# Behind the second attention: normalisation on ScalarE, single banks for the MLP's first product, its differences at the end, Gelu's table at the start

## The chip, the cores and the metric

The kernel runs on one core of one Trainium2 chip. The metric is device time in microseconds, from several executions; a profiled execution comes with a trace of every instruction of the five engines (TensorE is PE, its weight loads PEld; VectorE is DVE; ScalarE is ACT; GpSimd is POOL; SyncE, SP, issues most transfers). Everything is float32.

## What is computed

An input of 16 images with 256 channels and 32x32 pixels, so 1024 tokens an image, goes through two layers. Cut to what matters:

```python
# layer 0: attention, 4 heads of 64, with a residual
qkv = xs @ w_proj + b_proj
x = softmax(q @ k.T * 64**-0.5) @ v @ w_out + b_out + xs
# layer 1: group_norm, attention with 8 heads of 32, group_norm, MLP
x = x + attention(group_norm(x, gn1_w, gn1_b))
h = group_norm(x, gn2_w, gn2_b)
h = gelu(mlp_w1 @ h + mlp_b1)          # 256 -> 1024
x = x + mlp_w2 @ h + mlp_b2            # 1024 -> 256
```

A group norm has 32 groups of 8 channels; the softmax runs without subtracting a maximum, and a check of the denominators at the end decides whether a general version has to run as well. It doesn't run with these inputs.

## The kernel before

**Layout.** Channels lie on the 128 partitions in two chunks (CC = 2), tokens along the free dimension in two halves of 512 (NT = 2). [...]three double tiles `s0`, `s1`, `s2` (`wide`, L289) and two single banks `b0`, `b1` (`bank`, L295). `wide` without a number takes the double tile that was used longest ago, except for those in `kept`.

**One image.** The loop at L1089 handles image b in two stages, and each stage also carries work of a neighbouring image:

- The first attention (`attention_a`, L376). It has four items, (query half t, channel chunk c), with eight key blocks each. For every key block PE makes scores (L390), ACT their exponentials (L398), PE the weighted values two blocks later (L411), and DVE adds the exponentials up (`es`, L423); the first tile of an item is held and added together with the second, so that an item has seven adds. At an item's end ACT copies one half of the result (L427) and DVE adds the other (L428). During the fourth item the scores alternate between `s0` and `s1`, since `s2` holds the item's result. When both items of a half are done, `normalise` (L435) makes the denominators on PE (`den_a`, L442), which go out to memory as a row, are inverted, and come back (`denominators`, L349); `scale` (L462) multiplies the result by them. `out_proj` (L652) follows: product, residual (L663) and statistics (L666).
- Within that stage, after the first half's denominators, comes the rest of the image before: the last projection of its second attention (`j`), the statistics, and the second `group_norm` (L690, key `h`). `averages` (L695) averages over a group by PE; `apply` (L730) makes a factor `a` and an offset `c` per channel and applies them by four DVE operations (L746), one per half and chunk. `sums_of_input` (L868) then makes five sums and differences of the four blocks on DVE (L875 to L879).
- After the attention, `hidden` (L945): the first product of the MLP of the image before. It uses seven products for a two-by-two block product where eight are usual (Strassen's way). For each i of four, `begin` makes products 2 and 5 in a double tile and product 1 in a bank of its own (`once`), ACT copies one with a minus (L923), DVE makes `rest` (L924, L925); `middle` adds products 4 and 3 and takes two Gelus; `finish` adds 7 and 6, DVE makes two units (L938, L939), ACT takes two Gelus (L911), and `combine` (L951, operation at L954) makes two differences of units. The parts run as begin 0, begin 1, middle 0, middle 1, finish 0, finish 1, and the same for 2 and 3. The first group norm of this image (key `g`) and the second half of its projection (`o`) lie between them.
- Then the first products of the second attention (`qkv_1`, L822) and the second attention (`attention_b`, L500), which is filled up with the remaining products of `qkv_1`, the MLP's second product of the image before (`outputs`, `reduce`, L974) and the first products of the next image. The differences of units are read there.

**Order.** Every engine works through a queue whose order is fixed before the kernel runs. A planner makes that order: it takes what is ready by its own reckoning of time, and of several ready instructions the one written earlier. `tc.keep_in_program_order` ties an instruction behind the one written before it on the same engine. `Later` (L31) delays the writing of a step by a number of steps of the loop, so that a result that is long in coming is not waited for. The variable `cols` (L331) is 32 while an attention is being written and 128 (P) outside it, so `cols[0] == P` tells the group norm `g`, and the very last `h`, from the other fifteen `h`.

Of the kernel before, what the change touches and what calls it, by code (L numbers as in the profile page):

```python
# [8 lines left out]
F32 = mybir.dt.float32  # L9
I32 = mybir.dt.int32  # L10
AF = mybir.ActivationFunctionType
ALU = mybir.AluOpType
AX = mybir.AxisListType

P = 128
# [223 lines left out]
def first_pass(ctx, tc, x, out, k):  # L239
    nc = tc.nc  # L240
    B, C, S = x.shape
# [6 lines left out]
    small = ctx.enter_context(tc.tile_pool(name="small", bufs=2))  # L248
# [36 lines left out]
    def use(n):  # L285
        order.remove(n)
        order.append(n)

    def wide(name, n=None):  # L289
        if n is None:  # L290
            n = next(m for m in order if m not in kept)
        use(n)
        return ps_s.tile([P, 2, TB], F32, tag=f"s{n}", name=name)

    def bank(name, n):  # L295
        return ps_a.tile([P, TB], F32, tag=f"b{n}", name=name)
# [34 lines left out]
    cols = [P]  # L331

    def product(o, w, r, **flags):
        for c0 in range(0, P, cols[0]):
            sl = slice(c0, c0 + cols[0])
            nc.tensor.matmul(o[sl], w[:, sl], r, **flags)  # L336
# [353 lines left out]
    def group_norm(key, src, stats, gw, gb, tag, out_tile, wait, then=None):  # L690
        st = {}

        def averages(name, src):  # L695
            if cols[0] == P:
                ps = bank(name, 1)
                product(ps[:, :CC], k["gavg"], src, start=True, stop=True)
                return [(slice(0, P), ps[:, :CC])]
            ps = wide(name)  # L700
            halves = [slice(h, h + HALF) for h in range(0, P, HALF)]
            for n, sl in enumerate(halves):
                nc.tensor.matmul(
                    ps[sl, n, :CC], k["gavg"][sl, sl], src[sl], start=True, stop=True
                )
            return [(sl, ps[sl, n, :CC]) for n, sl in enumerate(halves)]

        def means():
            mv = small.tile([P, CC, 2], F32, tag="mv", name=f"mv_{key}")
            for cc in range(CC):  # L710
                nc.vector.bn_aggr(mv[:, cc, :], stats[:, cc].rearrange("p t k -> p (t k)"))
            mean_c = small.tile([P, CC], F32, tag="mean_c", name=f"mean_c_{key}")
            nc.vector.tensor_copy(mean_c, mv[:, :, 0])
            st.update(mv=mv, mean_c=mean_c)
            later.after(wait, variances)

        def variances():
            mean = small.tile([P, CC], F32, tag="mean", name=f"mean_{key}")
            for sl, ps in averages(f"gm_{key}", st["mean_c"]):
                nc.vector.tensor_copy(mean[sl], ps)  # L720

            dv = small.tile([P, CC], F32, tag="dv", name=f"dv_{key}")
            nc.vector.tensor_sub(dv, st["mean_c"], mean)
            nc.vector.tensor_mul(dv, dv, dv)
            tv = small.tile([P, CC], F32, tag="tv", name=f"tv_{key}")
            nc.vector.tensor_add(tv, dv, st["mv"][:, :, 1])
            st.update(mean=mean, tv=tv)
            later.after(1 if cols[0] == P else 2, apply)

        def apply():  # L730
            rstd = small.tile([P, CC], F32, tag="rstd", name=f"rstd_{key}")
            for sl, ps in averages(f"gv_{key}", st["tv"]):
                nc.vector.tensor_scalar(rstd[sl], ps, EPS, None, ALU.add)
            nc.gpsimd.tensor_tensor(rstd, rstd, k["mhalf"], ALU.pow)
            a = small.tile([P, CC], F32, tag="ga", name=f"ga_{key}")
            nc.vector.tensor_mul(a, rstd, gw)
            ma = small.tile([P, CC], F32, tag="gma", name=f"gma_{key}")
            nc.vector.tensor_mul(ma, st["mean"], a)
            c = small.tile([P, CC], F32, tag="gc", name=f"gc_{key}")
            nc.vector.tensor_sub(c, gb, ma)  # L740
            y = act.tile([P, CC, S], F32, tag=tag, name=f"gn_{key}")
            out_tile.append(y)
            for t in range(NT):
                sl = slice(t * TB, (t + 1) * TB)
                for cc in range(CC):
                    nc.vector.tensor_scalar(  # L746
                        y[:, cc, sl], src[:, cc, sl],
                        a[:, cc : cc + 1], c[:, cc : cc + 1], ALU.mult, ALU.add,
                    )
            if then:  # L750
                then(y)

        means()
# [114 lines left out]
    def sums_of_input(b, y):  # L868
        extra = act.tile([P, 3, TB], F32, tag="hs", name=f"hs_{b}")
        y11, y12 = (y[:, 0, t * TB : (t + 1) * TB] for t in range(NT))  # L870
        y21, y22 = (y[:, 1, t * TB : (t + 1) * TB] for t in range(NT))
        s1, s6, s7 = (extra[:, n] for n in range(3))
        inputs[b] = {1: s1, 2: y11, 3: y12, 4: y21, 5: y22, 6: s6, 7: s7}
        todo = [
            lambda: nc.vector.tensor_add(s1, y11, y22),  # L875
            lambda: nc.vector.tensor_add(s7, y21, y22),
            lambda: nc.vector.tensor_sub(y21, y21, y11),
            lambda: nc.vector.tensor_add(s6, y11, y12),
            lambda: nc.vector.tensor_sub(y12, y12, y22),  # L879
        ]  # L880
        for n, fn in enumerate(todo):
            if b < B - 1:
                later.after(1 + n, fn)
            else:
                fn()

    def mlp(b, xb):
        n4 = HC // 2
        gs, open_sums = {}, {}
# [6 lines left out]
        def products_of(i, to):  # L896
            for number, ps, first in to:
                nc.tensor.matmul(  # L898
                    ps, blocks[1][number - 1][:, i * P : (i + 1) * P],
                    inputs[b][number], start=first, stop=True, skip_group_check=not first,  # L900
                )

        def unit(half, t, i):
            gs[half, t, i] = work.tile(
                [P, TB], F32, tag="g", name=f"g_{b}_{half}_{t}_{i}", bufs=16
            )
            return gs[half, t, i]

        def gelu(half, t, i, what):
            hc = half * n4 + i  # L910
            nc.scalar.activation(  # L911
                gs[half, t, i], what, AF.Gelu, bias=k["m1b"][:, hc : hc + 1]
            )

        def begin(i):
            ps = wide(f"m1_{b}_{i}")
            if i % 2 == 0:
                open_sums["once"] = wide(f"m1_{b}_{i}_1")
            once = open_sums["once"][:, i % 2, :]
            open_sums[i] = ps  # L920
            products_of(i, [(2, ps[:, 0, :], True), (5, ps[:, 1, :], True), (1, once, True)])
            minus, rest = unit(0, 1, i), unit(1, 1, i)
            nc.scalar.activation(minus, ps[:, 0, :], AF.Copy, scale=-1.0)  # L923
            nc.vector.tensor_sub(rest, minus, ps[:, 1, :])  # L924
            nc.vector.tensor_add(rest, rest, once)  # L925
# [8 lines left out]
        def finish(i):  # L934
            ps = open_sums.pop(i)
            products_of(i, [(7, ps[:, 0, :], False), (6, ps[:, 1, :], False)])
            rest = gs[1, 1, i]
            nc.vector.tensor_add(unit(0, 0, i), rest, ps[:, 0, :])  # L938
            nc.vector.tensor_add(rest, rest, ps[:, 1, :])  # L939
            gelu(0, 0, i, gs[0, 0, i])  # L940
            gelu(1, 1, i, rest)
            combine((1, 0), (0, 0), False, i)
            combine((0, 1), (1, 1), False, i)

        hidden = [  # L945
            lambda part=part, i=i: part(i)
# [4 lines left out]
        def combine(to, what, plus, only=None):  # L951
            for i in range(n4) if only is None else (only,):
                d = gs[(*to, i)]
                (nc.vector.tensor_add if plus else nc.vector.tensor_sub)(  # L954
                    d, d, gs[(*what, i)]
                )

# [96 lines left out]
    ps, n = bank("bqk", 0), brow.shape[0]  # L1056
# [32 lines left out]
    for b in range(B):  # L1089
# [3 lines left out]
        if b:  # L1093
# [4 lines left out]
                lambda st, b=b, xn=xn: group_norm(  # L1098
                    f"g{b}", xs[b], st, k["g1w"], k["g1b"], "res", xn, 2 if b else 3
                ),  # L1100
# [13 lines left out]
        n = len(qk) // CC  # L1114
# [29 lines left out]
        for m, pieces in enumerate(rest):  # L1144
# [5 lines left out]
                lambda st, b=b, hn=hn: group_norm(  # L1150
                    f"h{b}", xs[b], st, k["g2w"], k["g2b"], "q1", hn,
                    *((3 if b + 1 < B else 1), lambda y, b=b: sums_of_input(b, y)),
                ),
            ),
            fill,
        )
        run_pieces(end)
        hidden, outputs = mlp(b, xs[b])
    later.flush()
    run_pieces(hidden + outputs)  # L1160
# [306 lines left out]
```

## Time and profile before

| | us |
|---|---|
| median of 3 runs (3698.66 to 3700.75) | 3700.3 |
| the profiled execution | 3700.63 |
| its span, first to last instruction | 3698.8 |
| around the span | 1.8 |
| DVE busy | 2688.2 (73%) |
| ACT busy | 2118.4 (57%) |
| POOL busy | 121.1 (3%) |

The granted TensorE clock is 0.999 over the whole span. An image takes 228.6 us: the second half's `den_a` starts at 738.83, 967.42 and 1196.00 us in three images that follow each other. Times below are those of one image, from 929 to 1043 us of the span. A float32 matmul is recorded as two instructions; back to back, 128x128x512 instructions start every 0.43 us (983.12 to 986.55 for eight).

### The profile page before, as it was taken

How to read it: one execution, taken by the hardware profiler on the slowest of the kernel's cores; microseconds unless marked ns; L12 is line 12 of the kernel's file. 1: busy time of each engine (PE TensorE's matmuls, PEld its weight loads, DVE VectorE, ACT ScalarE, POOL GpSimd, SP SyncE). 2: the span in 40 equal slices, each digit the busy share in tenths (PEclk: the TensorE clock that was granted, in tenths of full speed). 3: DMA queues.
4: the chain of work that ended last, by engine and by line, in shares of the span. 5: the costliest groups of instructions: out<-in, count | busy, mean ns of one | idle time of the engine just before them, and what ended most of it. 6: DMA issues, size and time to landing. Idle time of an engine off the chain costs nothing.

```text
span 3698.8 us, 79399 instructions
## 1 busy us (share of the span) xinstructions
PE 3644.9 (99%) x34221; PEld 1290.8 (35%) x34221; DVE 2688.2 (73%) x3486; ACT 2118.4 (57%) x2768; POOL 121.1 (3%) x266
## 2 busy tenths in 40 slices
PE   9999999999999999999999999999999999999999
PEld 4333333333333333333333333333333333333333
DVE  4686767767677776777777777787777877677777
ACT  4665646556565665646656465564655656556572
POOL 3000000000000000000000000000000000000000
PEclk9999999999999999999999999999999999999999
DMA  4000110101101011010110101001010010101100
GB/s 146 11 16 30 53 33 13 50 30 53 33 14 50 30 53 33 19 49 28 50 33 19 50 27 50 32 19 50 27 56 27 23 46 33 50 27 42 36 28 27
DMA packets 66548, 138.35 MB, mean 37 GB/s; under 512 B 35630, under 2 KB 36398, under 8 KB 61966
## 3 DMA queue, kind: packets, MB, share of 16 engines
q1 hardware_dynamic: 63116, 126.64, 10.7%
q8 instruction: 270, 4.42, 0.5%
q0 software_dynamic: 1328, 6.17, 0.5%
q14 instruction: 88, 0.72, 0.1%
q10 hardware_dynamic: 1746, 0.40, 0.1%
HBM read 111.17 MB, written 21.23 MB: 36 GB/s over the span
## 4 chain that ended last, share of the span: by engine, by line
PE 81%; DVE 14%; issue 3%; DMA 1%; ACT 1%; POOL 1%; SPq 0%; DVEq 0%; ACTq 0%
PE s_b L524 12%; PE acc_b L576 12%; PE m L336 10%; PE s_a L390 9%; PE acc_a L411 8%; PE m L898 6%; PE qk_a L336 6%; PE qk_b L336 5%; DVE es_a L423 4%; PE v_a L336 3%; PE j L336 3%; PE v_b L336 2%; PE den_b L598 1%; DVE g L954 1%; DVE es_b L555 1%
## 5 line engine op out<-in xcount | busy, mean ns | idle before, releaser
L539 ACT ACTIVATE e_b<-s_b 128x1024 f32<-128x1024 f32 (+1 forms) x1280 | 983.0, 864 | 151.0 <-PE s_b L524 151.0
L555 DVE TENSOR_TENSOR es_b<-es_b,e_b 128x1024 f32<-128x1024 f32 x768 | 899.1, 1218 | 217.3 <-ACT e_b L539 217.2
L398 ACT ACTIVATE e_a<-s_a 128x1024 f32<-128x1024 f32 x512 | 521.3, 1025 | 360.1 <-PE s_a L390 345.7
L524 PE MATMUL s_b<-q,k 32*64 32x512 f32 x8192 | 526.9, 601 | 9.8 <-DVE v L793 7.0
L390 PE MATMUL s_a<-q,k 64*64 64x512 f32 x4096 | 532.6, 593 | 1.1
L411 PE MATMUL acc_a<-e_a,v 64*64 64x512 f32 x4096 | 528.5, 589 | 0.0
L423 DVE TENSOR_TENSOR es_a<-es_a,e_a 128x1024 f32<-128x1024 f32 x384 | 471.0, 1226 | 58.4 <-ACT e_a L398 39.1
L576 PE MATMUL acc_b<-e_b,v 128*32 128x512 f32 x4096 | 493.8, 600 | 0.0
L336 PE MATMUL m<-g,w 128*32 128x512 f32 (+1 forms) x3320 | 404.3, 592 | 0.0
L524 PEld LDWEIGHTS s_b<-q,k 32*64 32x64 f32 x8192 | 166.1, 130 | 337.3 <-issue 127.7
L411 PEld LDWEIGHTS acc_a<-e_a,v 64*64 64x64 f32 x4096 | 161.9, 133 | 277.5 <-issue 236.1
L390 PEld LDWEIGHTS s_a<-q,k 64*64 64x64 f32 x4096 | 152.6, 133 | 278.1 <-issue 208.2
L898 PE MATMUL m<-gn_h,w 128*128 128x512 f32 x512 | 243.7, 604 | 5.7 <-DVE g L924 3.3
L589 DVE TENSOR_TENSOR res_b<-res_b,acc_b 128x512 f32<-128x512 f32 x192 | 131.6, 686 | 145.5 <-PE acc_b L576 145.5
L336 PE MATMUL qk_b<-gn_g,wq 128*32 128x512 f32 (+1 forms) x1280 | 235.7, 594 | 1.7
L576 PEld LDWEIGHTS acc_b<-e_b,v 128*32 128x32 f32 x4096 | 108.6, 109 | 358.2 <-ACT e_b L539 194.8
L336 PE MATMUL qk_a<-x,wp 128*32 128x512 f32 (+1 forms) x1856 | 233.5, 592 | 0.0
L336 PEld LDWEIGHTS m<-g,w 128*32 128x32 f32 (+1 forms) x3320 | 121.4, 112 | 262.3 <-issue 235.0
L954 DVE TENSOR_TENSOR g<-g,g 128x512 f32<-128x512 f32 x320 | 206.0, 680 | 4.0 <-ACT g L911 2.8
L898 PE MATMUL m<-hs,w 128*128 128x512 f32 x384 | 177.9, 592 | 0.1
L555 DVE TENSOR_TENSOR es_b<-e_b,e_b 128x1024 f32<-128x1024 f32 x128 | 150.6, 1217 | 0.0
L911 ACT ACTIVATE g<-g,m1b 128x512 f32<-128x512 f32 x128 | 92.1, 722 | 99.6 <-DVE g L938 72.7
(146 smaller groups left out, 2793.5 us busy)
## 6 DMA issues: line engine op xcount, KB each, us to landing
w<-w_kept SPq DMA_DIRECT2D x30, 1792.0 KB
d_a<-row_a SPq DMA_DIRECT2D x64, 256.0 KB
rd_b<-row_b SPq DMA_DIRECT2D x252, 64.0 KB
out_dram<-x SPq DMA_DIRECT2D x63, 256.0 KB
x<-in_x_dram SPq DMA_DIRECT2D x30, 512.0 KB
w_kept<-w_made POOLq DMA_DIRECT2D x2, 1792.0 KB, 7.1
w_made<-in_L_conv_mlp_w_dram POOLq DMA_DIRECT2D x8, 256.0 KB, 6.5
x<-in_x_dram SPq DMA_DIRECT2D x4, 256.0 KB
```

Source lines behind the costliest of these rows:

```text
L336: nc.tensor.matmul(o[sl], w[:, sl], r, **flags)
L390: nc.tensor.matmul(s[h : h + HALF, g, :], kT[g * D : (g + 1) * D, c, kb * P + h : kb * P + h + HALF], qT[g * D : (g + 1) * D, c, t * TB : ...
L398: nc.scalar.activation(e, s, AF.Exp, scale=float(D) ** -0.5)
L411: nc.tensor.matmul(accs[i][h][g * D : (g + 1) * D, :], v[h * HALF : (h + 1) * HALF, kb, c * 2 + g], e[h * HALF : (h + 1) * HALF, g, :], st ...
L423: nc.vector.tensor_add(sums[i], held[i] if kb == 1 else sums[i], e)
L524: nc.tensor.matmul(outs[g][h : h + HALF, :], kT[g * D : (g + 1) * D, c, k0 : k0 + HALF], qT[g * D : (g + 1) * D, c, t * TB : (t + 1) * TB] ...
L539: nc.scalar.activation(to, s, AF.Exp, scale=float(D) ** -0.5)
L555: ins = nc.vector.tensor_add(d, es[n % 2] if kb == 0 else d, es[n])
L576: nc.tensor.matmul(acc[g * D : (g + 1) * D, :], v[:, kb + m, c * G + g], es[2 * m + g // 2][:, g % 2, :], start=(m == 0), stop=(m == 1),)
L589: nc.vector.tensor_add(r, r, acc)
L898: nc.tensor.matmul(ps, blocks[1][number - 1][:, i * P : (i + 1) * P], inputs[b][number], start=first, stop=True, skip_group_check=not first,)
L954: (nc.vector.tensor_add if plus else nc.vector.tensor_sub)(d, d, gs[(*what, i)])
```

## The change

It has four parts.

- `apply`: where `cols[0]` isn't P, the four DVE operations become four ACT activations (Identity with `a` as scale and `c` as bias).
- `begin`: the double tile is fixed as `s0` for an even and `s1` for an odd i, and `once` goes to the single bank `b0` or `b1`. `averages` goes from bank `b1` to the double tile `s2`.
- `finish` and `combine`: the eight differences of an image are written behind the last `finish`, apart from those of the last image, and each is tied into program order.
- `begin(0)`: a Gelu of one column is written first, tied into program order, so that the table for Gelu is loaded there.

```diff
         def averages(name, src):
             if cols[0] == P:
-                ps = bank(name, 1)
+                ps = wide(name, 2)[:, 0, :]
...
                 for cc in range(CC):
-                    nc.vector.tensor_scalar(
-                        y[:, cc, sl], src[:, cc, sl],
-                        a[:, cc : cc + 1], c[:, cc : cc + 1], ALU.mult, ALU.add,
-                    )
+                    if cols[0] == P:
+                        nc.vector.tensor_scalar(
+                            y[:, cc, sl], src[:, cc, sl],
+                            a[:, cc : cc + 1], c[:, cc : cc + 1], ALU.mult, ALU.add,
+                        )
+                    else:
+
+                        nc.scalar.activation(
+                            y[:, cc, sl], src[:, cc, sl], AF.Identity,
+                            bias=c[:, cc : cc + 1], scale=a[:, cc : cc + 1],
+                        )
...
         def begin(i):
-            ps = wide(f"m1_{b}_{i}")
-            if i % 2 == 0:
-                open_sums["once"] = wide(f"m1_{b}_{i}_1")
-            once = open_sums["once"][:, i % 2, :]
+            if i == 0:
+
+                few = small.tile([P, 1], F32, tag="few", name=f"few_{b}")
+                tc.keep_in_program_order(
+                    nc.scalar.activation(few, k["mhalf"][:, :1], AF.Gelu)
+                )
+            ps, once = wide(f"m1_{b}_{i}", i % 2), bank(f"m1_{b}_{i}_1", i % 2)
...
-            combine((1, 0), (0, 0), False, i)
-            combine((0, 1), (1, 1), False, i)
+
+            for n in (i,) if b == B - 1 else range(n4) if i == n4 - 1 else ():
+                combine((1, 0), (0, 0), False, n)
+                combine((0, 1), (1, 1), False, n)
...
-                (nc.vector.tensor_add if plus else nc.vector.tensor_sub)(
+                ins = (nc.vector.tensor_add if plus else nc.vector.tensor_sub)(
                     d, d, gs[(*what, i)]
                 )
+                if not plus:
+                    tc.keep_in_program_order(ins)
```

## The prediction

> **What bounds the kernel now.** I read the page first, then PE's list of waits, then the order of time of each engine in one image.
>
> ```profile
> span 3698.8 us, 79399 instructions
> PE 3644.9 (99%) x34221; PEld 1290.8 (35%) x34221; DVE 2688.2 (73%) x3486; ACT 2118.4 (57%) x2768; POOL 121.1 (3%) x266
> ...
> PE den_a L442 <- DVE res_a L428: 28.1, 15, 1.9
> PE s_b L524 <- DVE v L793: 7.0, 16, 1.2
> PE m L898 <- DVE g L924: 3.3, 15, 1.0
> ```
>
> PE is busy 3644.9 of 3698.8 us, so all idle time together is 54 us, and a change that leaves PE's work alone can win little more. Over half of the idle time is one wait: in 15 images of 16 the second denominators wait 1.9 us for DVE's add of the result. What makes DVE late there shows in its order of time (start, duration, line, operation, number; in brackets idle time before it):
>
> ```profile
> 950.88 0.16 DVE L740 TENSOR_TENSOR gc_h<-g2b,gma_h 128x2 f32<-128x2 f32 x1
> 951.08 1.92 DVE L746 TENSOR_SCALAR gn_h<-x,ga_h,gc_h 128x512 f32<-128x512 f32 x4
> 952.91 0.68 DVE L878 TENSOR_TENSOR hs<-gn_h 128x512 f32<-128x512 f32 x1
> ...
> 955.92 1.22 DVE L423 TENSOR_TENSOR es_a<-e_a,e_a 128x1024 f32<-128x1024 f32 x1
> 957.16 0.69 DVE L428 TENSOR_TENSOR res_a<-res_a,acc_a 128x512 f32<-128x512 f32 x1
> 957.77 1.22 DVE L468 TENSOR_TENSOR res_a<-res_a,d_a 128x1024 f32<-128x1024 f32 x1
> 958.90 7.87 DVE L423 TENSOR_TENSOR es_a<-es_a,e_a 128x1024 f32<-128x1024 f32 x6
> 966.69 0.68 DVE L428 TENSOR_TENSOR res_a<-res_a,acc_a 128x512 f32<-128x512 f32 x1
> ...
> 967.42 1.07 PE L442 MATMUL den_a<-es_a,ones 128*32 128x256 f32 x16 [1.87 <-DVE res_a L428]
> ```
>
> From 951.08 to 966.69 no line has idle time before it: normalisation, five sums, the fourth item's adds, one after another. The first image has no normalisation of a predecessor there, and its DVE idles before the last add; it is the one image without the wait. So DVE time between 951 and 967 counts one for one, until PE's own end of work at 965.4 (o from 963.62, four steps of 0.43) comes last.
>
> The other place is the MLP's first product:
>
> ```profile
> 983.12 3.60 PE L336 MATMUL o<-res_a,wo 128*128 128x512 f32 x8
> 986.55 3.60 PE L898 MATMUL m<-gn_h,w 128*128 128x512 f32 x8
> 990.31 1.13 PE L898 MATMUL m<-gn_h,w 128*128 128x512 f32 x2 [0.16 <-DVE g L924]
> ...
> 998.86 2.41 PE L336 MATMUL qk_b<-gn_g,wq 128*128 128x512 f32 x5
> ```
>
> From 986.55 to 998.86 PE has 26 instructions of 0.43 (11.16) and two tiny averages (0.28), so 11.44 us of work in 12.31: 0.87 us an image is lost to DVE, partly inside what counts as busy.
>
> [...]L923 (a constant scale) 597, L772 (a bias) 688; Gelu with a bias from SBUF takes 722. No row has two operands. [...]Identity at L772 runs between exponentials, and the only loads are 16 at L911, 15 at L539 and one at the start. [...]L746 takes 542 ns, the two-source L875 684. So the operation moved is a cheap one on DVE and a dearer one on ACT.
>
> **Normalisation on ACT.** Removed from DVE: 1.83 us (951.08 to 952.91). [...]
>
> The operands come at 951.04, so ACT can start at 951.1; the third ends 2.26 later at 953.4, the fourth at 954.1. The first sum, L878, needs the third block, and the next needs the fourth. DVE meets these sums before the fourth item's adds. So L878 starts at 953.4 instead of 952.9: DVE does not work on the normalisation any more, but waits for it. Second sum 954.1, third 954.7, end of the DVE chain 0.6 later than before (0.1 with 600 ns).
>
> On ACT the four stand in a queue with the exponentials:
>
> ```profile
> 948.87 1.02 ACT L398 ACTIVATE e_a<-s_a 128x1024 f32<-128x1024 f32 x1 [0.81 <-PE s_a L390]
> 950.95 1.02 ACT L398 ACTIVATE e_a<-s_a 128x1024 f32<-128x1024 f32 x1 [1.05 <-PE s_a L390]
> 951.87 0.58 ACT L427 COPY res_a<-acc_a 128x512 f32<-128x512 f32 x1
> 952.60 1.02 ACT L398 ACTIVATE e_a<-s_a 128x1024 f32<-128x1024 f32 x1 [0.16 <-PE s_a L390]
> ```
>
> These are the fourth item's first exponentials. Two score tiles alternate here, so a late exponential stops PE two blocks on. *Behind the first one* (948.87): the second runs at 954.0 instead of 950.95, and PE's fourth scores, due at 953.22, start at 955.1: PE loses 1.85 us. But PE then reaches the denominators at 967.2, and DVE's chain ends at 967.42 plus 0.6: PE's loss lies under the wait, and the image loses 0.6. *Ahead of the first one*: ACT stands idle until 951.1, that exponential runs at 954.1 to 955.1, and PE's third scores, due at 951.50, start 3.65 late; PE comes to the denominators at 969.0, 1.6 late, and now PE is last. *Behind the second one*: the second add can run on DVE while ACT normalises, and the image loses 0.2.
>
> Which of these holds is the planner's choice and not in the trace. It can be narrowed down: the five sums stand ahead of the add at 955.92, whose exponential had ended at 951.97, so the plan reckons PE slower than it is; yet the copy of the means at 942.88 stands behind the add at 941.79, so not much slower. Both fit a plan in which a block's scores take 1.6 to 2.0 us (they take 0.86), with the first exponential ready slightly ahead of the operands. I take "behind the first": plus 0.6, times 15 is plus 9 us (bounds 0.1 and 0.7: plus 1.5 to plus 10).
>
> **Single banks and late differences.** Before, begin 2's `once` could run early, ahead of `o`, and filled 0.86 us for which PE would otherwise wait for L468. Now `b0` is first taken by `o`. In exchange begin 2 and 3 have all six products at hand. Step by step: finish 1 ends at 982.26 on PE; L468 (from 980.75, 1.23) has ended at 982.0; `o` runs 982.26 to 985.7. The differences between 983.92 and 989.6 (four, 0.6 each) are gone from DVE, so L939 of unit 1 runs at 983.8 instead of 985.79, both residuals leave `b0` and `b1` at 985.2 and 986.6, and the means are ready near 987.9 instead of 990.3. Begin 2 and 3 run from 985.7 to 990.85; L924 is done by 989, so the 0.16 us of bracketed wait goes. Normalisation `g` ends near 994 instead of 997.4, L939 of unit 2 near 997.5, before PE comes to `qk_b`. With no stall `qk_b` would start at 998.0: 0.86 won. L468's margin is 0.2 us and one image's transfer is 2 us late, so I take 0.75, times 15 is minus 11 us (bounds 0.3 and 0.86: minus 4.5 to minus 13). The eight differences (5 us) then follow L939 of unit 3, from 1000.1 to 1005.1; the next DVE work, L793 at 1007.75, had 4.92 us of idle time before it, which is their cover; without it PE's scores would wait for them one for one. They are not read before the MLP's second product, near 1040.
>
> **Early table, averages in `s2`, the last image.** The load (1.28 us) moves from 975.35 into ACT's idle 3.02 us before 972.16; the Gelu behind it waited for PE anyway, so nothing changes. `s2` is free by then, as `den_a` was copied out at 968.56. In the last image a begin waits for L1009 (1.3 us, once), which fixed tiles could spare or not: minus 0.5.
>
> **Sum.** Plus 9, minus 11, minus 0.5 is minus 2.5 us. Against the profiled execution's 3700.6, which stands 0.3 above the median, this gives 3698.
>
> **Rivals.** *ACT stands idle for the operands* (slower). It is decided by one place in ACT's queue: the four ahead of the fourth item's first exponential. It costs 1.6 an image, 25 us; less 11 it gives 3714. It turns from harmless to dear once PE's stall exceeds some 2.5 us, the wait plus what DVE is late. For it speaks that the plan reckons PE slow; against it, that the operands pass through seven small steps (949.35 to 951.04, GpSimd among them). *DVE fills its wait* (faster): if adds stand before the sums, up to 0.9 us of the 1.87 goes (DVE is idle at least from 951.04 to 952.0, when the second exponential ends, out of 1.83 removed). 0.9 times 15 is 13; with 11 from the MLP 3676; the plain form, behind the second exponential, 3692. Against it speaks that the sums stood ahead of that add before. *The MLP wins nothing*, because the new bank order makes PE wait elsewhere: plus 9 alone, 3709.
>
> **How the numbers follow.** Forecast 0.42 (own range 3689 to 3705), idle ACT 0.28, filled DVE 0.22, no win in the MLP 0.08. This measurement can tell about 0.2% (7.4 us) from no change. Faster: 0.19 of the filled case, 0.07 of the forecast's lower end. Slower: 0.25 of idle ACT, 0.05 of no win, 0.03 of the forecast. The rest, 0.41, is the same. The range reaches from the filled case to idle ACT with the upper end of its costs: 3677 to 3717.
>
> **What would show it.** The four activations behind one exponential of the fourth item, about 720 ns apart; DVE idle some 2.3 us before L878; `den_a`'s wait in the list shrunk to under 1 us an image, with a new wait of s_a for ACT of near 1.8; `den_a` no earlier after 951 than before; 11.5 us instead of 12.3 from `o`'s end to `qk_b`. It is wrong if `den_a` starts over 1 us earlier or later relative to the operands at 951.04, or if the stretch of the MLP isn't shorter.

## The result and the profile after

The changed kernel takes 3731.6 us, the median of four runs (3729.34 to 3733.22), against 3700.3 for the kernel before: the ratio is 1.0085 with an interval of [1.0068, 1.0102]. It is slower, and outside the range that was given. The profiled execution has a span of 3731.4 us where the one before had 3698.8, so 32.6 us have to be found.

The page of the changed kernel, its busy times and the group of the first attention's scores:

```profile
span 3731.4 us, 79416 instructions
PE 3658.1 (98%) x34221; PEld 1293.5 (35%) x34221; DVE 2678.5 (72%) x3426; ACT 2158.7 (58%) x2844; POOL 120.9 (3%) x266
L390 PE MATMUL s_a<-q,k 64*64 64x512 f32 x4096 | 542.4, 602 | 50.1 <-ACT e_a L398 49.3
```

The same group in the kernel before:

```profile
L390 PE MATMUL s_a<-q,k 64*64 64x512 f32 x4096 | 532.6, 593 | 1.1
```

PE's waits in the changed kernel (in total, times, longest):

```profile
PE s_a L390 <- ACT e_a L398: 49.3, 15, 3.3
PE s_b L524 <- DVE v L800: 7.0, 16, 1.2
PE o L336 <- DVE res_a L468: 3.0, 15, 0.2
```

Two things are to be seen. The wait of the denominators for DVE, 28.1 us before, is gone from the list, and one of 49.3 us stands in its place: in 15 images the scores wait 3.3 us for ACT. And PE is busy 13.2 us longer (3658.1 against 3644.9) with as many instructions, so some of them took longer.

ACT's order of time in the same image (the changed lines lie a little lower in the file: the activation is L753, the sums L882 to L886, the first product L905, the first unit L948):

```profile
952.10 1.02 ACT L398 ACTIVATE e_a<-s_a 128x1024 f32<-128x1024 f32 x1 [0.69 <-PE s_a L390]
956.13 2.93 ACT L753 ACTIVATE gn_h<-x,gc_h,ga_h 128x512 f32<-128x512 f32 x4 [3.00 <-DVE gc_h L740]
958.96 1.91 ACT L398 ACTIVATE e_a<-s_a 128x1024 f32<-128x1024 f32 x2
```

The exponential at 952.10 is the last of the third item. The four activations stand next in the queue, *ahead* of the fourth item's first exponential, and their operands come at 956.1. ACT is idle for 3.00 us, works 2.93 us on the four, and only at 958.96 takes the exponentials, two in one go because both scores had long been there.

PE in that stretch, changed kernel:

```profile
955.69 1.04 PE L411 MATMUL acc_a<-e_a,v 64*64 64x512 f32 x8
960.01 1.35 PE L390 MATMUL s_a<-q,k 64*64 64x512 f32 x8 [3.28 <-ACT e_a L398]
961.12 1.95 PE L411 MATMUL acc_a<-e_a,v 64*64 64x512 f32 x8
962.82 1.69 PE L390 MATMUL s_a<-q,k 64*64 64x512 f32 x8
964.34 1.04 PE L411 MATMUL acc_a<-e_a,v 64*64 64x512 f32 x8
```

PE stands for 3.28 us before the fourth item's third scores. Then comes what no line of the page says: eight instructions that usually take 1.04 us together take up to 1.95. Four stretches of 3.41 us in two images show why (columns: window, its length, busy time and number of instructions of PE, PEld, DVE, ACT, POOL, then the granted TensorE clock, DMA share, GB/s):

```profile
957.29:960.70 3.41, 0.69 (x8) 0.36 (x12) 2.30 (x4) 3.41 (x5) 0.00 (x0) 1.00 0.00 0
960.70:964.11 3.41, 3.41 (x20) 1.07 (x16) 3.38 (x5) 1.66 (x3) 0.00 (x0) 0.50 0.03 7
...
725.21:728.62 3.41, 1.80 (x16) 0.36 (x12) 0.48 (x3) 2.21 (x4) 0.58 (x1) 1.00 0.00 0
728.62:732.03 3.41, 1.74 (x16) 0.67 (x20) 3.35 (x6) 3.41 (x6) 0.00 (x0) 1.00 0.00 0
```

From 960.70 to 964.11 the granted clock is half. All stretches at half clock in the images of this trace last 3.413 us and start on one grid of 3.413 us (starts at 960.7, 1192.8 and 1653.6, for example, are 68 and 135 steps apart). In this image 2.72 of the 3.28 us of idle time fell into one step of the grid, and the next step ran at half clock. In the image before, at 725 to 732 us, the same idle time lay across two steps, each with over 1.7 us of work, and nothing was slowed.

So the images come in two kinds. From the first half's denominators to the second half's (the starts of `den_a`) it is 32.96 us before; after, 34.40 in five images and 36.10 in ten. The first kind is plus 1.44, the second plus 3.14, and the 1.70 between them is half a grid step, the work that a step at half clock leaves undone. Ten times 3.14 and five times 1.44 are 38.6 us. From the second denominators to the next image's first it is 195.32 instead of 195.63; over all images, with one late transfer in the trace of before (1.7 us in one image), that is minus 5.6. Together plus 33.0, of the 32.6 to be found.

### The profile page after: what moved, and what is told of

It reads as the page before. It is cut to its first block, busy times and chain, and to the rows that moved or that the text cites. A ratio compares the mean times of both kernels' runs of the same rounds, so it can differ in the third digit from the quotient of the medians.

```text
span 3731.4 us, 79416 instructions
## 1 busy us (share of the span) xinstructions
PE 3658.1 (98%) x34221; PEld 1293.5 (35%) x34221; DVE 2678.5 (72%) x3426; ACT 2158.7 (58%) x2844; POOL 120.9 (3%) x266
## 4 chain that ended last, share of the span: by engine, by line
PE 92%; DVE 3%; issue 2%; ACT 2%; DMA 1%; SPq 0%; POOL 0%; DVEq 0%; ACTq 0%
PE s_b L524 12%; PE s_a L390 12%; PE acc_b L576 12%; PE acc_a L411 11%; PE m L336 10%; PE m L905 10%; PE qk_a L336 6%; PE qk_b L336 5%; PE o L336 3%; PE v_a L336 3%; PE j L336 3%; PE v_b L336 2%; PE den_b L598 1%; DVE es_b L555 1%; ACT gn_h L753 1%
## 5 line engine op out<-in xcount | busy, mean ns | idle before, releaser
L390 PE MATMUL s_a<-q,k 64*64 64x512 f32 x4096 | 542.4, 602 | 50.1 <-ACT e_a L398 49.3
L411 PE MATMUL acc_a<-e_a,v 64*64 64x512 f32 x4096 | 537.5, 598 | 0.0
L336 PE MATMUL m<-g,w 128*32 128x512 f32 (+1 forms) x3320 | 404.2, 592 | 0.0
L905 PE MATMUL m<-gn_h,w 128*128 128x512 f32 x512 | 239.8, 601 | 1.1 <-DVE gn_h L747 0.6
L336 PE MATMUL qk_b<-gn_g,wq 128*32 128x512 f32 (+1 forms) x1280 | 234.8, 593 | 0.0
L336 PE MATMUL qk_a<-x,wp 128*32 128x512 f32 (+1 forms) x1856 | 233.7, 592 | 0.5 <-ACT k L779 0.5
L336 PEld LDWEIGHTS m<-g,w 128*32 128x32 f32 (+1 forms) x3320 | 121.5, 112 | 262.2 <-issue 235.5
L905 PE MATMUL m<-hs,w 128*128 128x512 f32 x384 | 180.4, 592 | 0.1
L798 ACT COPY v<-v_a 128x512 f32<-128x512 f32 x64 | 37.5, 585 | 180.6 <-PE v_a L336 180.6
```

The source lines that it names most:

```text
L390: nc.tensor.matmul(s[h : h + HALF, g, :], kT[g * D : (g + 1) * D, c, kb * P + h : kb * P + h + HALF], qT[g * D : (g + 1) * D, c, t * TB : ...
L411: nc.tensor.matmul(accs[i][h][g * D : (g + 1) * D, :], v[h * HALF : (h + 1) * HALF, kb, c * 2 + g], e[h * HALF : (h + 1) * HALF, g, :], st ...
L905: nc.tensor.matmul(ps, blocks[1][number - 1][:, i * P : (i + 1) * P], inputs[b][number], start=first, stop=True, skip_group_check=not first,)
```

## The experiments

### Each half of the change by itself

**The normalisation back on VectorE, all else as changed:**

```diff
-                    if cols[0] == P:
-                        nc.vector.tensor_scalar(...)
-                    else:
-                        nc.scalar.activation(...)
+                    nc.vector.tensor_scalar(...)
```

> The changed kernel with its first part undone: the second group norm is applied by VectorE again, the other three parts stay. Theory Q (the place in ScalarE's queue ahead of the fourth item's first exponential costs all of it): the time falls below the kernel before by what the MLP's first product won in the changed kernel, 0.31 us an image by the two traces, so 3700 - 5 = 3695; the wait of den_a for VectorE is back at 1.9 us in 15 images. Rival B (the single banks or the late differences cost): the time stays above 3715.

Measured: 3693.5 us, ratio to the kernel before 0.9983 [0.9976, 0.9990]. The old wait is back in PE's list:

```profile
PE den_a L442 <- DVE res_a L428: 28.1, 15, 1.9
```

**The normalisation on ScalarE alone, on the kernel before:**

```diff
+                    if cols[0] == P:
                         nc.vector.tensor_scalar(...)
+                    else:
+                        nc.scalar.activation(...)
```

> The kernel before with the first part alone: the second group norm is applied by ScalarE. Theory Q: 3700 + 37 = 3737 (1.44 us an image from one denominator to the next in all 15 images, and 1.7 more in each image in which the clock is halved, 9 in the changed kernel), with waits of s_a for e_a of 3.3 us. Rival B: about 3700 to 3710.

Measured: 3741.3 us, 1.0108 [1.0091, 1.0125]. Eleven images lost a grid step to the half clock here, and the mean granted clock is 0.994 (ten images and 0.995 in the changed kernel, where I had counted nine for what was expected); in one of them the slow step began before PE's stall was over, and a second followed it. The loss is all in the normalisation, and the rest of the change wins some 6 us by itself.

### Is it the place in the queue, and what does the clock take?

**The four activations behind the fourth item's first exponential** (the form that was forecast), all else as changed. They are written one step of the loop later and tied into program order; the sums behind them are written one step later too, but not tied:

```diff
+            def on_scalar(t, cc):
+                tc.keep_in_program_order(nc.scalar.activation(...))
...
+                for wait, (t, cc) in zip((1, 1, 1, 1), blocks4):
+                    later.after(wait, lambda t=t, cc=cc: on_scalar(t, cc))
+                if then:
+                    later.after(1, lambda: then(y))
```

> The changed kernel with the four activations of the second group norm written one step later and tied behind the fourth item's first exponential. Theory Q: ScalarE no longer stands idle with an exponential ready, PE's wait for e_a falls to 1.85 us, which is hidden in the wait for the denominators, no halved clock; from one denominator to the next 32.96 + 0.6 = 33.6 us; 3700 + 9 - 5 = 3704. Rival C (the 2.9 us of ScalarE's work cost, wherever they stand): PE's wait stays near 3 us and the time above 3720.

Measured: 3699.7 us, 1.0000 [0.9991, 1.0008]. ACT in that image of this experiment:

```profile
947.25 1.02 ACT L398 ACTIVATE e_a<-s_a 128x1024 f32<-128x1024 f32 x1 [0.81 <-PE s_a L390]
949.45 2.93 ACT L746 ACTIVATE gn_h<-x,gc_h,ga_h 128x512 f32<-128x512 f32 x4 [1.17 <-DVE gc_h L740]
952.28 1.00 ACT L398 ACTIVATE e_a<-s_a 128x1024 f32<-128x1024 f32 x1
```

and PE's waits:

```profile
PE s_a L390 <- ACT e_a L398: 23.6, 15, 1.6
PE den_a L442 <- DVE res_a L428: 6.2, 15, 0.4
```

PE stands 1.6 us at the scores (1.85 had been worked out), most of it under what had been the denominators' wait, of which 0.4 is left: the image loses 0.33 us against the kernel before, 0.6 had been worked out. None of the fifteen images loses clock at this place (the mean granted clock is 0.999). One exponential moved ahead of the four activations is worth 32 us.

**Eight more matmuls in PE's stall**, in the changed kernel, ahead of the fourth item's third scores. Their results go to a tile that the kernel overwrites afterwards, and nothing is left out:

```diff
             s = wide(f"s_{key}_{i}_{kb}")
+            if b and i == len(items) - 1 and kb == 2:
+                early.append(wide(f"acc_{key}_{i}", 2))
+                for g in range(4):
+                    for h in range(0, P, HALF):
+                        nc.tensor.matmul(early[0][h : h + HALF, g % 2, :], ...)
```

> The changed kernel with eight more matmuls (1.7 us of PE) just ahead of the fourth item's third scores, the place where PE waits 3.3 us for ScalarE; their results are overwritten. Theory Q with the clock as a cost of its own: PE's idle time there falls to 1.6 us, the clock is halved in no image, ScalarE's times don't move, and the time falls by 9 times 1.7 = 15 us to 3716. Rival: the halved clock has another cause, or costs nothing; then the time stays at 3731 or rises.

Measured: 3716.6 us, 1.0046 [1.0029, 1.0062], which is 15.0 us less than the changed kernel for *more* work. All fifteen images take 34.40 us from denominators to denominators, and PE's wait at this place is 1.6 us where it was 3.3 (the lines of this kernel lie lower in its file):

```profile
PE s_a L402 <- ACT e_a L410: 23.5, 15, 1.6
```

The exponentials come no earlier, since ACT stands idle for its operands as long as before:

```profile
952.90 2.93 ACT L765 ACTIVATE gn_h<-x,gc_h,ga_h 128x512 f32<-128x512 f32 x4 [3.00 <-DVE gc_h L752]
```

What has gone is the half clock: no step ran at it before the last 3 us of the span, and the mean granted clock is 1.000 where it was 0.995. Ten steps of 1.70 us are 17 us; the medians differ by 15.0, the two profiled spans by 18.2 (3731.4 and 3713.2). What was expected had come to 15 by counting nine images, so its agreement to a tenth is chance. The prediction's rival "ACT stands idle" had put the cost at 1.6 us an image; with the clock held it is 1.44.

### Where the MLP's gain comes from

**Single banks alone** (the changed `begin` without its Gelu, and `averages` in `s2`, on the kernel before):

```diff
-            ps = wide(f"m1_{b}_{i}")
...
+            ps, once = wide(f"m1_{b}_{i}", i % 2), bank(f"m1_{b}_{i}_1", i % 2)
```

> The kernel before with the second part alone (fixed double tiles and single banks for the MLP's first product, averages in s2). If the 0.27 us an image between the second denominators and qk_b come from the banks (six products at hand), 31.44 becomes 31.2 us or less; if they come from the late differences, it stays at 31.4 or grows, because the early product that filled PE ahead of o is gone.

Measured: 3700.1 us, 1.0002 [0.9993, 1.0011]. The second half's `o` starts 14.84 us after the denominators, 0.86 earlier than before, but `qk_b` 31.38 after, only 0.06 earlier. Behind `o` stands one product more (0.86 us), and `qk_b` now waits for one of DVE's units, a wait that PE's list of the kernel before does not have:

```profile
PE qk_b L336 <- DVE g L936: 7.3, 15, 0.5
```

**Late differences alone** (`finish` and `combine` of the change, on the kernel before):

```diff
-            combine((1, 0), (0, 0), False, i)
-            combine((0, 1), (1, 1), False, i)
+            for n in (i,) if b == B - 1 else range(n4) if i == n4 - 1 else ():
+                combine((1, 0), (0, 0), False, n)
+                combine((0, 1), (1, 1), False, n)
```

> The kernel before with the third part alone (the eight differences behind the last finish, tied). If the gain comes from the late differences (VectorE reaches the residuals and the means 1.2 us or more sooner), 31.44 us from denominators to qk_b becomes 31.0 to 31.2; if it comes from the banks, it stays at 31.4.

Measured: 3689.6 us, 0.9974 [0.9963, 0.9985]. `qk_b` comes 30.76 us after the denominators where it was 31.44. All of the gain is here, 0.68 an image, and it lies behind `o`, which starts 15.70 us after the denominators as before. With the banks and the early table added, in the first experiment, `qk_b` comes at 31.20.

**The early table alone** (the Gelu of one column, on the kernel before):

```diff
+            if i == 0:
+                few = small.tile([P, 1], F32, tag="few", name=f"few_{b}")
+                tc.keep_in_program_order(
+                    nc.scalar.activation(few, k["mhalf"][:, :1], AF.Gelu)
+                )
```

> The kernel before with the fourth part alone, Gelu of one column ahead of the MLP's first product. The load moves into ScalarE's idle time and nothing waits for it before or after: the same time within 0.1%, all stretches as before.

Measured: 3701.8 us, 1.0006 [0.9998, 1.0014]. No change in time that can be told, but in the trace `qk_b` comes 31.73 us after the denominators, 0.29 later: the planner made another order. DVE has the unit (L938 before, L943 here) ahead of L468, where before it stood behind, and PE has three products ahead of `gv_g` where it had two. `qk_b` then waits 0.49 us for DVE's last unit (`PE qk_b L336 <- DVE g L944: 7.3, 15, 0.5` in PE's list). That this order belongs to the new instruction, which takes ACT's time in the plan, is an inference.

### Moving the sums instead

The wait that the change was to shorten comes from DVE's chain ahead of the second denominators, and the five sums in it are not read before PE's products on `hs`. So they can go behind it.

**The five sums with the second denominators**, the normalisation on VectorE, all else as changed:

```diff
             if b < B - 1:
-                later.after(1 + n, fn)
+                later.after(10, lambda fn=fn: tc.keep_in_program_order(fn()))
```

> The kernel of e1_norm_on_dve (normalisation on VectorE, the other three parts kept) with the five sums of the MLP's input taken out of the fourth item: they are written when the second denominators are, tied into program order, so the adds of the fourth item come right behind the normalisation. Theory V (VectorE's time between the operands and the last add counts one for one until PE's own work is last): 3.0 us less of it, the wait of den_a falls from 2.36 to 0.3 us, 32.96 becomes 30.9 us between denominators, 15 times 2.06 = 31 us; at most 10 us given back behind the denominators, where the sums now stand; 3662 to 3672. Rival: the sums are only moved to another place where PE waits for them, and the time stays near 3693.

Measured: 3660.8 us, 0.9898 [0.9881, 0.9914]. 30.90 us from denominators to denominators; the wait is gone, and PE's own work is the limit. DVE's last add, which now waits for ACT's copy, and PE's denominators, with no idle time before them:

```profile
955.28 0.69 DVE L428 TENSOR_TENSOR res_a<-res_a,acc_a 128x512 f32<-128x512 f32 x1 [0.62 <-ACT res_a L427]
956.26 1.05 PE L442 MATMUL den_a<-es_a,ones 128*32 128x256 f32 x16
```

**The same with the normalisation on ScalarE, its four activations one step apart**, each tied behind an exponential of the fourth item:

```diff
+                for wait, (t, cc) in zip((2, 3, 4, 5), blocks4):
+                    later.after(wait, lambda t=t, cc=cc: on_scalar(t, cc))
```

> As e5_sums_late, but the normalisation is done by ScalarE as in the change, its four activations written one step apart, each tied behind an exponential (the first behind the second exponential of the fourth item). If only the place in the queue made the change's first part dear, this is within 0.2% of e5_sums_late, with no wait of s_a for e_a above 0.5 us and no halved clock. If ScalarE's 2.9 us cost wherever they stand, it is over 15 us slower than e5_sums_late.

Measured: 3661.1 us, 0.9900 [0.9883, 0.9916], no different from the one before, and 30.89 us from denominators to denominators. Each of the four stands by itself between two exponentials, the first of them as

```profile
943.40 0.83 ACT L746 ACTIVATE gn_h<-x,gc_h,ga_h 128x512 f32<-128x512 f32 x1
```

The four activations cost nothing when they wait for nothing and hold nobody up. They win nothing either once the sums are out of the way.

**Late sums and late differences on the kernel before**, without banks and table:

> The kernel before with two moves alone: the differences behind the last finish (as e8_differences_alone) and the five sums behind the second denominators (as e5_sums_late); normalisation on VectorE, tiles and banks as before, no early table. If the single banks cost 0.3 us an image beside the late differences (195.2 against 194.9 us from the second denominators to the next first), this is 5 us faster than e5_sums_late: 30.9 us between denominators, 194.9 to the next, 3656. If the two moves get in each other's way, 3661 or more.

Measured: 3661.9 us, 0.9897 [0.9882, 0.9913]; that is the second of the two cases that were expected, 6 us above the first. In this experiment's DVE order:

```profile
970.18 0.69 DVE L938 TENSOR_TENSOR g<-g,m 128x512 f32<-128x512 f32 x1 [4.46 <-PE m L898]
970.79 1.22 DVE L468 TENSOR_TENSOR res_a<-res_a,d_a 128x1024 f32<-128x1024 f32 x1
```

and in PE's:

```profile
972.06 3.70 PE L336 MATMUL o<-res_a,wo 128*128 128x512 f32 x8 [0.20 <-DVE res_a L468]
```

The planner put the first unit of the MLP (L938) ahead of L468, and DVE stood 4.46 us idle for it, while `o` needs L468.

**The same with unit 0 tied behind L468:**

```diff
-            nc.vector.tensor_add(unit(0, 0, i), rest, ps[:, 0, :])
+            ins = nc.vector.tensor_add(unit(0, 0, i), rest, ps[:, 0, :])
+            if i == 0:
+                tc.keep_in_program_order(ins)
```

> As e10_two_moves, with unit 0's first addition (L938) tied behind what is written before it on VectorE, L468 among it, as the queue stood in the kernel before. If the 0.33 us from denominators to o in e10_two_moves (16.03 instead of 15.70) come from L938 standing ahead of L468, o starts at 15.70 again, qk_b at 30.8 instead of 31.21, 6 us less: 3655. If not, 3661.

Measured: 3656.2 us, 0.9880 [0.9863, 0.9896], the best of all, and faster than both kernels. DVE in one image of it:

```profile
943.91 1.22 DVE L423 TENSOR_TENSOR es_a<-e_a,e_a 128x1024 f32<-128x1024 f32 x1
...
946.90 7.87 DVE L423 TENSOR_TENSOR es_a<-es_a,e_a 128x1024 f32<-128x1024 f32 x6
955.38 0.69 DVE L428 TENSOR_TENSOR res_a<-res_a,acc_a 128x512 f32<-128x512 f32 x1 [0.62 <-ACT res_a L427]
...
958.01 0.68 DVE L875 TENSOR_TENSOR hs<-gn_h 128x512 f32<-128x512 f32 x1
...
969.99 1.23 DVE L468 TENSOR_TENSOR res_a<-res_a,d_a 128x1024 f32<-128x1024 f32 x1 [3.93 <-DMA d_a<-row_a]
971.13 0.68 DVE L938 TENSOR_TENSOR g<-g,m 128x512 f32<-128x512 f32 x1
```

The adds follow the normalisation, and the last add at 955.38 waits for ACT's copy of PE's result instead of making PE wait; the sums come at 958.01; L468 is released by its transfer and not by a unit of the MLP.

**The same tie on the version with single banks and early table:**

> As e5_sums_late, with the same tie. With the single banks PE has no early product ahead of o, so o starts as soon as L468 has ended: 14.8 instead of 16.58 us behind the denominators; qk_b at 30.7 instead of 31.08 if nothing else waits, 5 us less: 3655. If the means or L924 then end last, 31.0 and 3660.

Measured: 3663.5 us, 0.9899 [0.9883, 0.9916]: no gain over 3660.8, a miss. Here DVE and PE have

```profile
971.71 1.22 DVE L468 TENSOR_TENSOR res_a<-res_a,d_a 128x1024 f32<-128x1024 f32 x1 [4.71 <-DMA d_a<-row_a]
```

```profile
972.99 3.70 PE L336 MATMUL o<-res_a,wo 128*128 128x512 f32 x8 [0.41 <-DVE res_a L468]
```

With single banks, PE comes to `o` one product (two instructions, 0.86 us) sooner, before the denominators are back from memory; L468 was free to go and had nothing to work on. The product that covered this transfer now stands behind `o`, where it covers nothing. So these traces put the loss to the single banks; that the early table has no part in it is not shown, as no run has the tie with the banks and without the table.

## Why the prediction was wrong

**The step that failed is "I take 'behind the first': plus 0.6."** The four activations stand ahead of the fourth item's first exponential. The form that I forecast was measured by the third experiment: plus 0.33 an image instead of 0.6, PE's stall 1.6 instead of 1.85, and 3699.7 us in all, inside the forecast's own range. The cost of that form was right within 0.3 us an image; its place in the queue was not. That the 3699.7 lie within 2 us of my 3698 is in part luck: the activations cost some 4 us less than I had said, and the MLP won some 6 us less. I narrowed the place down from the plan's reckoning of a block's scores, on two orders that both allowed either case, and gave the rival 0.28. Evidence that allows both cases chooses neither.

**The rival "ACT stands idle" held, with a term missing.** It said the third scores would start 3.65 us late and the image lose 1.6. Recorded: a stall of 3.28 and, where the clock held, 1.44. Its 3714 lacked the clock: ten images lost another 1.70 us, 17 us in sum, and the eight matmuls put into the stall took 15.0 us of it back. My sum had no price for the clock. Before the last 3 us of its span, the trace of before shows a single step at half clock, in the last image (the last section has it).

**The durations were right.** The 720 ns from start to start were my estimate; the trace of before shows nearly that for Gelu alone (three of L911, of 722 ns each, in 2.15 us from 982.61 on, so 0.71 from start to start). The four take 798 ns each and 2.93 us in all, 0.71 from start to start, and L885 started 2.29 us after DVE's last step, where I had said some 2.3. That DVE would wait for the normalisation in place of doing it was right. The list "what would show it" was wrong on the wait of s_a (3.3 instead of 1.8) and on `den_a`. By my own sign the forecast was wrong there: counted from the operands, `den_a` starts at 19.54 us in the image shown (956.09 to 975.63) and 1.70 less in the images that kept their clock, where it was 16.38 before (951.04 to 967.42), so over 1 us later in both kinds.

**The MLP's term was mis-sized: 0.75 forecast, 0.31 measured** (31.44 to 31.18 up to `qk_b` in the changed kernel, 195.63 to 195.32 up to the next image). The sum took `o` at 982.26, right behind finish 1, with L468 ended 0.2 us earlier: 14.84 us after the denominators, with `qk_b` 15.74 behind it. Measured are 15.18 and 16.00, so of the 0.86 won in the sum 0.34 is missing ahead of `o` and 0.26 behind it. With the banks alone `o` comes as the sum has it (14.84). In the changed kernel it doesn't, as its DVE shows,

```profile
988.93 0.69 DVE L948 TENSOR_TENSOR g<-g,m 128x512 f32<-128x512 f32 x1 [3.90 <-PE m L905]
989.53 1.22 DVE L468 TENSOR_TENSOR res_a<-res_a,d_a 128x1024 f32<-128x1024 f32 x1
```

and its PE:

```profile
990.80 3.70 PE L336 MATMUL o<-res_a,wo 128*128 128x512 f32 x8 [0.20 <-DVE res_a L468]
994.34 1.88 PE L905 MATMUL m<-gn_h,w 128*128 128x512 f32 x4
...
1006.80 5.37 PE L336 MATMUL qk_b<-gn_g,wq 128*128 128x512 f32 x12
```

The unit stands ahead of L468, so `o` is 15.18 us behind the denominators. This is the activations' fault once more, on DVE: an operation with a late operand stands ahead of a ready one. Untied, the planner did so in the changed kernel, with the table alone and with the two moves. I had spoken of L468's margin as a matter of its transfer, not of its place.

Behind `o` my working contradicts itself: the sum has 12.3 us from `o`'s end to `qk_b` (985.7 to 998.0), the list of signs 11.5, which leaves out the product that moved from ahead of `o` to behind it. The trace has 12.46 (994.34 to 1006.80), so this stretch did not become shorter than its 12.31 of before, which by my own sign was wrong as well; the 0.26 won at `qk_b` lie ahead of `o`.

The late differences gave 0.68 as a part. The single banks, which I had credited with making the products handy, gave 0.06 alone; banks and table together took back 0.44 beside late differences (30.76 to 31.20), and how much of that belongs to each is open.

**The early table "changes nothing"**: right in the time, though not in the order that the planner made.

**The bound was right.** PE's idle time of 54 us limited what could be won: with both moves and the tie the kernel wins 44 us, 31 of them at the wait that the prediction showed as the largest (32.96 to 30.90, 15 times).

## What to carry to other kernels

When an operation moves to another engine, price its place in that engine's queue before its duration: what stands behind it waits for its operands too; here one exponential moved ahead of the four activations was worth 32 us (3731.6 to 3699.7). If the trace of before can't show the place, tie it in the order that you want, or give both places their full weight. When a chain is too long for a wait, look first for links in it that nobody needs yet: moving the five sums back won 33 us (3693.5 to 3660.8) with no other engine at work. And price an idle gap of PE by where it may fall on the clock's grid as well as by its length: the same 3.28 us brought a step at half clock, 1.70 us of lost work, in ten images and none in five.

## What the runs showed of the hardware

Half clock came here without a step in which PE was idle throughout. Over all fourteen kernels' traces (from 200 to 3480 us, the steps with over 1.3 us of PE idle) each step of 3.413 us in which PE had been idle for some 2.1 us or more, 22 of them, was followed by a step at half clock, and none of the more than 90 with 1.89 us or less was. The idle time here is worked out from the matmuls' starts and modelled ends. A single wait of 2.2 us was followed by it too. In the traces of the banks alone and of the differences alone, DVE stood half a microsecond between two adds in two images each, for no reason that the trace shows, and the wait at the denominators grew from 1.87 to 2.2 us. Three of these four images lost clock too; in the fourth the wait lay across two steps. By this count the old wait of 1.87 us had been just short of it.

But idle time alone is not what decides. In the first image and the last, outside the stretch counted, seven of the traces have a step with only 1.2 us of idle time, at the wait of the second attention's scores for `v`, and the next step at half clock. The kernel before is one of them (columns as above):

```profile
3539.84:3543.26 3.42, 2.21 (x28) 0.49 (x20) 3.35 (x4) 2.92 (x4) 0.00 (x0) 1.00 0.00 0
3543.26:3546.67 3.41, 3.41 (x20) 0.87 (x20) 0.00 (x0) 1.02 (x1) 0.00 (x0) 0.50 0.00 0
```

The same wait in its first image, with as much idle time in the step from 140.16 (2.20 us of work in 3.41), was followed by a step at a granted clock of 1.00. So the limit near 2 us holds for the places where this change acts; what the clock goes by besides is open.

ACT kept to the order of its queue: in the changed kernel it stood idle for 3.00 us before four activations whose operands had not come, with an exponential ready behind them.

And a dearer operation cost nothing: four activations of 0.83 us each in place of 1.83 us of DVE changed the time by 0.01% (3661.1 against 3660.8) once nothing waited behind them.
